# A new order for layer 0's hand-written table, and k's first product ahead of q's in layer 1

## The chip, the cores and the metric

The kernel runs on one core of a Trainium2 chip. The metric is the device time of one execution in microseconds (us). The engines are PE (TensorE, matrix products), DVE (VectorE), ACT (ScalarE), POOL (GpSimd) and SP (SyncE, which here only issues transfers). Each runs its own instructions in the order in which they were built, and waits for the others by semaphores.

## The reference, cut to what matters

Two transformer layers act on x of shape 4 x 512 x 512 in float32. Each is modulated by a row vector c:

```python
mod = (_silu(L0_c) @ L0_wmod).reshape(L0_c.shape[0], 6, 1, -1)
sa, ca, ga, sb, cb, gb = (mod[:, 0], mod[:, 1], mod[:, 2], mod[:, 3], mod[:, 4], mod[:, 5])
h = _layernorm(x, axis=-1) * (1 + ca) + sa
x = x + ga * _L0_attn_ref(h, L0_attn_Wq, L0_attn_bq, L0_attn_Wk, L0_attn_bk, L0_attn_Wv, L0_attn_bv)
h = _layernorm(x, axis=-1) * (1 + cb) + sb
x = x + gb * _L0_ffn_ref(h, L0_ffn_weight, L0_ffn_bias, L0_ffn_centroids, L0_ffn_assignments)
```

Layer 0's attention is small: a softmax over the 16 head dimensions of each position, whose result is repeated over 32 heads. Its feed-forward part computes softmax scores against 64 centroids and keeps a dense product only where a score passes a threshold. Layer 1 has the same frame with causal attention (32 query heads of 128, 8 key and value heads) and a gated feed-forward part with integer weights. Layer 1 takes most of the time.

## The kernel before, in words

All work is cut into tiles of 128 partitions. The batch has four entries b, and each entry's x is held on the chip as four tiles t of 128 rows. The schedule of layer 0 and of the start of layer 1 is manual: every engine gets its instructions in the order in which Python issues them.

**Layer 0** is a class `Pieces` (L291) with one short method per step, and a string `order` (L666) that lists the steps. A name such as `T.1.0.2` calls the method `T` with the numbers 1, 0, 2. `/d` or `/p` moves a step to DVE or POOL. The loop at L709 calls them one by one. Which engine a step uses:

- SP issues loads: `c`, `x.b` (x.0 alone from ACT), `wm.l.j` (the six 1 MB parts j of layer l's modulation weights, three buffers), `wq`, `wkv`, `cent`, `wffn`, `b2`, `asg`; `gw` and `gs` store a gate row and load it back, spread over all partitions; `wl` (L333) closes the buffers of modulation, opens those of layer 1 and loads its first q, k, v and o weights.
- PE: `M.l.j` multiplies silu(c) by a part of the weights; `MT` and `G` turn the result into columns (4 columns out) or a row; `T.i.b.c` transposes a normalized chunk; `Q.b.t` is the q, k, v product of 48 columns; `oT` and `ad` bring the attention back to x; `L` are the centroid scores; `hit` and `rs` collect the selection; `F.b.t` is the dense product, eight 512-column passes and the bias.
- DVE: `st` and `ve` and `nm` are the statistics of a layernorm; `wcat`, `bcat` sum weights and biases over heads; `biasr` splits the bias; `gr` clips a gate row; `qe`, `s`, `mx`, `den`, `rec`, `os`, `o` are the small attention; `xa`, `lm`, `ld`, `qs`, `fs`, `cs`, `sel` are adds, centroid softmax and selection; `mo` stores a modulation column.
- ACT: `siluexp`, `xn` (normalizing), `exp`, `le`, `re`; and, unless marked otherwise, the evacuations `pc`, `ev`, `oe`.
- POOL: `pw` (the power that gives 1/deviation), `sub` and `mul` of the attention, `R` (gate times a mask), `asgf`, `fa` unless marked, and `wsq` (sums of q's weights).

The last argument pairs are b and t, except that T and ev have a chunk c, and M, MT, pc, mo, G, gr, gw, gs have layer and part. The i of T, st, xn, ev and nm is 1 or 2 for layer 0's two layernorms and 3 for layer 1's first. M, `ad` and `F` share three banks of PSUM, `MT`, `G`, `Q`, `L` two others, and `T`, `oT` two more. A product that finds its bank unread waits for the step that empties it.

**Layer 1** multiplies 2 x 2 blocks by seven products (L738) in place of eight. They need sums of blocks of each operand: `sums_in` (L250) for weights, on POOL, and `sums_h` (L764) for h, on POOL and DVE (T1, T2, T3, T4 at L242 to L245). The products go in the order `SEVENTH = (1, 6, 2, 5, 3, 7, 4)`; product 1 needs no sum, 6 needs T2 and the weights' third sum, 7 needs T3. `gather` (L772) adds each product into q, k or v by DVE, product 1 by ACT. Products use the three banks of M and F. Eight pieces `select` (L278, `sel`) are spread between the first products, and `put` stores x to DRAM.

Attention then goes by `window` (L1120): each takes eight score tiles (products, row maxima, exponentials, division, flip), works pieces of other products in between, and ends with `carry` (L911), 16 transfers that turn the probabilities. Window -1 scores the first pair of heads and has no value products. The first half of q's two tiles, which it scores, is complete after the products 1, 6, 2, 5 and 3.

Of the kernel before, what the change touches and what calls it, by code (L numbers as in the profile page):

```python
# [33 lines left out]
def adaln_two_layers(ctx: ExitStack, tc: tile.TileContext, a, out: bass.AP):  # L34
# [629 lines left out]


    order = """  # L666
    c x.0 wkv wm.0.0 wq wm.0.1 x.2 wm.0.2 siluexp cent x.1 x.3 silu st.1.0.0 bcat st.1.0.1
    st.1.0.2 st.1.0.3 ve.1.0 pw.1.0 M.0.0 nm.1.0 xn.1.0.0 xn.1.0.1 wm.1.0 pc.0.0/d xn.1.0.2
    MT.0.0 xn.1.0.3 wcat T.1.0.0 mo.0.0 T.1.0.1 M.0.1 wm.0.3 pc.0.1/d MT.0.1 st.1.2.0
    st.1.2.1 mo.0.1 st.1.2.2 ev.1.0.0 st.1.2.3 T.1.0.2 ev.1.0.1 ve.1.2 pw.1.2 M.0.2  # L670
    ev.1.0.2/d nm.1.2 T.1.0.3 wm.0.4 pc.0.2/d b2 G.0.2 xn.1.2.0 ev.1.0.3/d xn.1.2.1 Q.0.0
    gr.0.2 xn.1.2.2 Q.0.1 xn.1.2.3 T.1.2.0 Q.0.2 st.1.1.0 ev.1.2.0 gw.0.2 T.1.2.1 st.1.1.1
    Q.0.3 ev.1.2.1 st.1.1.2 T.1.2.2 st.1.1.3 gs.0.2.0 gs.0.2.1 T.1.2.3 ev.1.2.2 qe.0
    gs.0.2.2 ve.1.1 gs.0.2.3 s.0 pw.1.1 ev.1.2.3 M.1.0 nm.1.1 mx.0 xn.1.1.0 Q.2.0 wm.1.3
    xn.1.1.1 pc.1.0/d asg sub.0 xn.1.1.2 Q.2.1 st.1.3.0 xn.1.1.3 st.1.3.1 MT.1.0 exp.0
    st.1.3.2 M.0.3 mo.1.0 st.1.3.3 Q.2.2 wm.1.4 pc.0.3 den.0 T.1.1.0 Q.2.3 ve.1.3 ev.1.1.0
    mul.0 rec.0 M.0.4 biasr MT.0.3 wm.0.5 pc.0.4 R.0 wffn T.1.1.1 os.0 T.1.1.2 ev.1.1.1 R.1
    ev.1.1.2 T.1.1.3 mo.0.3 R.2 o.0 MT.0.4 qe.2 ev.1.1.3 s.2 oT.0 R.3 Q.1.0 oe.0 mo.0.4 mx.2
    pw.1.3 ad.0.0 Q.1.1 nm.1.3 asgf xa.0.0 xn.1.3.0 sub.2 M.1.3 xa.0.1 xn.1.3.1 st.2.0.0
    xn.1.3.2 ad.0.1 wm.1.5 st.2.0.1 xn.1.3.3 Q.1.2 onehot exp.2 xa.0.2 T.1.3.0 xa.0.3 Q.1.3  # L680
    pc.1.3 den.2 ev.1.3.0 M.1.4 st.2.0.2 MT.1.3 mul.2 wm.1.2 pc.1.4 st.2.0.3 T.1.3.1 M.0.5
    rec.2 ev.1.3.1 ve.2.0 qe.1 pw.2.0 T.1.3.2 os.2 wm.1.1 pc.0.5 MT.1.4 ev.1.3.2 nm.2.0
    T.1.3.3 o.2 mo.1.4 xn.2.0.0 oT.2 s.1 G.0.5 ev.1.3.3 mo.1.3 xn.2.0.1 gr.0.5 Q.3.0
    xn.2.0.2 Q.3.1 xn.2.0.3 oe.2 T.2.0.0 ad.2.0 mx.1 gw.0.5 ev.2.0.0 T.2.0.1 xa.2.0 sub.1
    Q.3.2 ev.2.0.1 xa.2.1 gs.0.5.0 T.2.0.2 gs.0.5.1 st.2.2.0 ad.2.1 gs.0.5.2 ev.2.0.2
    gs.0.5.3 st.2.2.1 T.2.0.3 exp.1 xa.2.2 M.1.2 xa.2.3 ev.2.0.3 Q.3.3 den.1 pc.1.2 L.0.0
    st.2.2.2 mul.1 M.1.1 rec.1 st.2.2.3 L.0.1 pc.1.1 qe.3 ve.2.2 M.1.5 os.1 pw.2.2 L.0.2
    nm.2.2 o.1 xn.2.2.0 s.3 oT.1 MT.1.1 xn.2.2.1 oe.1/d L.0.3 xn.2.2.2 mx.3 xn.2.2.3 ad.1.0
    pc.1.5/d sub.3 T.2.2.0 lm.0 F.0.0 ev.2.2.0 xa.1.0 le.0 xa.1.1 exp.3 st.2.1.0 den.3
    T.2.2.1 st.2.1.1 mul.3 ad.1.1 ev.2.2.1 mo.1.1 rec.3 T.2.2.2 ld.0 G.1.5 ev.2.2.2 T.2.2.3  # L690
    xa.1.2 hit.0 ev.2.2.3 G.1.2 xa.1.3 F.0.1 os.3 st.2.1.2 st.2.1.3 o.3 ve.2.1 gr.1.5 pw.2.1
    oT.3 F.0.2 oe.3 nm.2.1 gw.1.5 qs.0 xn.2.1.0 fs.0.0 xn.2.1.1 fs.0.1 fa.0.0/p L.2.0
    xn.2.1.2 fs.0.2 xn.2.1.3 ad.3.0 fa.0.1/p fa.0.2/d T.2.1.0 xa.3.0 L.2.1 ev.2.1.0 xa.3.1
    T.2.1.1 st.2.3.0 ad.3.1 ev.2.1.1 st.2.3.1 T.2.1.2 xa.3.2 L.2.2 ev.2.1.2 xa.3.3 T.2.1.3
    st.2.3.2 L.2.3 ev.2.1.3 st.2.3.3 F.0.3 gr.1.2 ve.2.3 gw.1.2 lm.2 pw.2.3 L.1.0 fs.0.3
    le.2 F.1.0 nm.2.3 fa.0.3/p ld.2 xn.2.3.0 wl xn.2.3.1 qs.2 xn.2.3.2 xn.2.3.3 L.1.1
    T.2.3.0 L.1.2 ev.2.3.0/d T.2.3.1 L.1.3 ev.2.3.1/d T.2.3.2 lm.1 hit.2 ev.2.3.2 T.2.3.3
    F.1.1 ev.2.3.3/d le.1 ld.1 qs.1 fs.1.0 L.3.0 fa.1.0/d fs.1.1 hit.1 L.3.1 fa.1.1/d F.1.2
    L.3.2 fs.1.2 F.1.3 fa.1.2/d L.3.3 fs.1.3 F.2.0 fa.1.3/d lm.3 le.3 ld.3 F.2.1 qs.3 fs.2.0
    fa.2.0/d hit.3 fs.2.1 F.2.2 cs fa.2.1/p rs fs.2.2 F.2.3 re fa.2.2/d sel.0.0 sel.0.1  # L700
    sel.0.2 sel.0.3 F.3.0 st.3.0.0 st.3.0.1 st.3.0.2 st.3.0.3 fs.2.3 F.3.1 ve.3.0 fa.2.3/p wsq
    fs.3.0 fa.3.0/d pw.3.0 nm.3.0 sel.2.0 sel.2.1 sel.2.2 sel.2.3 xn.3.0.0 xn.3.0.1 F.3.2 fs.3.1 xn.3.0.2 fa.3.1/d xn.3.0.3
    T.3.0.0 fs.3.2 T.3.0.1 ev.3.0.0 F.3.3 fa.3.2/d ev.3.0.1 T.3.0.2 fs.3.3 T.3.0.3 ev.3.0.2
    fa.3.3/d ev.3.0.3
    """.split()
# [791 lines left out]
```

## Time and profile before

| | us |
|---|---|
| median of 3 runs | 2056.61 (2055.76 to 2058.26) |
| the profiled execution | 2058.11 |
| its span on the core | 2056.2 |
| PE busy in the span | 2020.9 |
| DVE, ACT, POOL busy | 1362.9, 878.9, 756.9 |
| first product M starts | 11.89 |
| last dense product of layer 0 (F.3.3) ends | 187.8 |
| first score product starts | 209.68 |
| first value product starts | 238.81 |

The span runs from the core's first to its last instruction. In rows of the timeline the first number is the start, the second the duration, and brackets hold the idle time of the engine ahead of the row and what ended it. Ends of matmuls are modelled, so a busy PE may still work below its peak. The granted clock is the share of TensorE's full clock; before its first recorded change the trace shows 1.00.

### The profile page before, as it was taken

To read this page: it belongs to the slowest core of one execution; us is meant where nothing else is said; L and a number is where in the kernel's file an instruction comes from. 1 tells how busy PE (TensorE), PEld (TensorE's weight loads), DVE (VectorE), ACT (ScalarE), POOL (GpSimd) and SP (SyncE) were. 2 spreads that over 40 slices of the span, in tenths; PEclk is the share of its full clock that TensorE was granted. 3 is DMA by queue.
4 is the path that set the end of the run, shared out by engine and by line. 5 is a ranking of instruction groups with operands and counts; after the bars stand their busy time and mean duration, and the time that the engine had idled before them with its cause. 6 is when DMAs were issued, how large, how long until landed. Compare 5 with 4: busy or idle time off the path is not lost.

```text
span 2056.2 us, 27492 instructions
## 1 busy us (share of the span) xinstructions
PE 2020.9 (98%) x9219; PEld 1580.4 (77%) x9219; DVE 1362.9 (66%) x3323; ACT 878.9 (43%) x1998; POOL 756.9 (37%) x656
## 2 busy tenths in 40 slices
PE   6999999999999999999999999999999999999998
PEld 4655777878787887877787878787877777888887
DVE  6766776677667666766677676667666674655554
ACT  3421554445444444544444445444444454223322
POOL 2314234434336443353473334337333333800000
PEclk8799999999999999999999999999999999999999
DMA  8310656676657766655766665567656556600000
GB/s 299 123 62 30 173 151 175 159 175 153 144 144 192 180 160 161 164 144 152 186 182 163 154 164 133 144 154 177 167 144 154 141 128 202 196 21 1 21 21 22
DMA packets 243640, 288.59 MB, mean 140 GB/s; under 512 B 23250, under 2 KB 184018, under 8 KB 243492
## 3 DMA queue, kind: packets, MB, share of 16 engines
q1 hardware_dynamic: 242964, 285.71, 52.8%
q8 instruction: 76, 1.25, 0.3%
q10 hardware_dynamic: 528, 1.05, 0.2%
q14 instruction: 72, 0.59, 0.1%
HBM read 142.99 MB, written 11.57 MB: 75 GB/s over the span
## 4 chain that ended last, share of the span: by engine, by line
PE 94%; DVE 3%; ACT 1%; issue 1%; DMA 1%; POOL 0%; SPq 0%; DVEq 0%; ACTq 0%
PE quarter L746 46%; PE av L928 14%; PE sc L878 13%; PE p_gate L1347 5%; PE p_up L1347 5%; PE acc L1366 4%; PE ffn L634 2%; PE lnT L477 1%; PE modps L390 1%; PE lg L593 1%; PE qkv_ps L507 1%; PE modT_ps L403 1%; PE add_ps L578 1%; DVE bnst L60 0%; DMA c_sb<-in_L_cT_dram 0%
## 5 line engine op out<-in xcount | busy, mean ns | idle before, releaser
L878 PE MATMUL sc<-kT,qT 128*128 128x512 f32 (+3 forms) x1024 | 355.1, 433 | 0.0
L928 PE MATMUL av<-x,v 128*128 128x512 f32 x1008 | 295.7, 437 | 3.7 <-DMA x<-p 3.7
L928 PEld LDWEIGHTS av<-x,v 128*128 128x128 f32 x1008 | 190.3, 192 | 110.7 <-issue 66.5
L881 DVE TENSOR_REDUCE nmx<-sc 128x1 f32<-128x512 f32 (+3 forms) x512 | 251.6, 491 | 17.7
L893 ACT ACTIVATE x<-x,rden 128x512 f32<-128x512 f32 (+3 forms) x256 | 143.6, 561 | 235.4 <-DVE rden L892 235.4
L778 DVE TENSOR_TENSOR qT<-qT,quarter 128x512 f32<-128x512 f32 x224 | 150.5, 684 | 133.9 <-PE quarter L746 127.7
L893 ACT ACTIVATE p<-p,rden 128x512 f32<-128x512 f32 (+3 forms) x256 | 143.7, 561 | 221.5 <-DVE rden L892 219.8
L879 DVE TENSOR_TENSOR sc<-sc,mask 128x128 f32<-128x128 f32 x512 | 145.5, 284 | 136.5 <-PE sc L878 135.6
L842 DVE TENSOR_TENSOR acc<-acc,quarter 128x512 f32<-128x512 f32 x196 | 134.5, 686 | 134.6 <-PE quarter L746 134.4
L230 POOL TENSOR_TENSOR sq<-wq 128x512 f32<-128x512 f32 x32 | 40.6, 1269 | 471.5 <-DMA wq<-in_L_attn_w_q_dram 453.0
L878 PEld LDWEIGHTS sc<-kT,qT 128*128 128x128 f32 x1024 | 182.6, 191 | 24.2
L746 PEld LDWEIGHTS quarter<-wo,oT 128*128 128x128 f32 x744 | 140.9, 190 | 43.9 <-issue 20.1
L746 PE MATMUL quarter<-wo,oT 128*128 128x256 f32 x744 | 171.1, 379 | 0.2 <-ACT oT L933 0.2
L883 ACT ACTIVATE p<-sc,nmx 128x512 f32<-128x512 f32 (+3 forms) x256 | 135.1, 528 | 75.8 <-DVE nmx L881 67.1
L883 ACT ACTIVATE x<-sc,nmx 128x512 f32<-128x512 f32 (+3 forms) x256 | 134.9, 527 | 70.1 <-DVE nmx L881 65.4
L933 ACT COPY oT<-av 128x512 f32<-128x512 f32 x128 | 74.3, 581 | 167.0 <-PE av L928 165.0
L896 DVE STREAM_TRANSPOSE p<-p 128x512 f32<-128x512 f32 (+3 forms) x256 | 129.4, 506 | 2.0 <-ACT p L893 0.5
L896 DVE STREAM_TRANSPOSE x<-x 128x512 f32<-128x512 f32 x248 | 125.0, 504 | 1.3 <-ACT x L893 0.9
L746 PE MATMUL quarter<-hsum,sq 128*128 128x256 f32 x512 | 121.1, 379 | 1.4 <-DVE hsum L244 1.4
L746 PEld LDWEIGHTS quarter<-hT,wq 128*128 128x128 f32 x512 | 97.2, 190 | 32.4 <-issue 14.8
L746 PE MATMUL quarter<-hsum,wq 128*128 128x256 f32 x512 | 121.0, 379 | 0.0
L746 PE MATMUL quarter<-hT,wq 128*128 128x256 f32 x512 | 120.9, 379 | 0.0
(257 smaller groups left out, 3752.7 us busy)
## 6 DMA issues: line engine op xcount, KB each, us to landing
x<-p SPq DMA_DIRECT2D x512, 128.0 KB, 3.7
x<-x SPq DMA_DIRECT2D x496, 128.0 KB, 3.8
wq<-in_L_attn_w_q_dram SPq DMA_DIRECT2D x32, 1024.0 KB, 5.6
...
```

Of the source, the lines that this page charges most:

```text
L746: nc.tensor.matmul(ps[:, m, :], l[:, k, m * P : (m + 1) * P], r[:, k, :], start=(k == 0), stop=(k == 1),)
L778: nc.vector.tensor_tensor(c[out], c[v], ps, ADD if sign > 0 else SUB)
L842: nc.vector.tensor_tensor(osum[:, i - 1], osum[:, i - 1], ps, ADD)
L878: nc.tensor.matmul(ps[:, :w], q[:, i * P : w], kT[n][:, :w], start=True, stop=True)
L879: nc.vector.tensor_tensor(ps[:, i * P : w], ps[:, i * P : w], mask, ADD)
L881: nc.vector.tensor_reduce(nmx, ps[:, :w], AX.X, ALU.max, negate=True)
L883: nc.scalar.activation(blocks(s, i), ps[:, :w].rearrange("p (j q) -> p j q", q=BK), AF.Exp, bias=nmx, accum_out=den,)
L893: nc.scalar.mul(p, p, rden)
L896: nc.vector.transpose(blocks(s, i), blocks(s, i))
L928: nc.tensor.matmul(av.rearrange("p (a n) -> p a n", a=NG)[:, :, BK * k :], vs[n][:, k, :], pT[:, k, :, P * (s % 2) + BK * k : P * (s % 2 + ...
L1347: nc.tensor.matmul(ps[kind], w[kind][:, k, c * P : (c + 1) * P], h2[b % 2][i][:, k, :], start=(k == 0 and i == 0), stop=(k == KC - 1 and i ...
L1366: nc.tensor.matmul(acc[t], act[i][:, t * P : (t + 1) * P], w[:, c, :], start=(n == 0 and i == 0), stop=(n == NI - 1 and i == 1),)
```

## The change

Layer 0's table is replaced by another order of the same steps. Two products M now come first on PE, several evacuations change engine, and tiles t are taken in other orders. The first F pieces come earlier and some at the very end, behind the normalizing for layer 1. `wl` comes later, and a new step `wsk` sums k's weights inside the table, where only `wsq` was. Two lines in `st` and `xn` open a buffer at the first tile taken, whichever it is.

In layer 1 the first products are k's first, q's first, the other six of k, four of q. The last two of q go into window -1, ahead of v's seven. The stores of x of entries 3, 0 and 1 are issued ahead of the next weights' loads, and k's load and sums ahead of q's.

```diff
@@ -341,6 +341,9 @@
             for kind in ("q", "k", "v", "o"):
                 load(kind, 0)
 
+        def wsk(self):
+            sums_in("k", 0)
+
         def wsq(self):
             sums_in("q", 0)
 
@@ -442,7 +445,7 @@
 
 
         def st(self, i, b, t):
-            if t == 0:
+            if ("st", i, b) not in T:
                 T["st", i, b] = moments()
             statistics(b, t, *T["st", i, b])
 
@@ -463,7 +466,7 @@
             )
 
         def xn(self, i, b, t):
-            if t == 0:
+            if ("xn", i, b) not in T:
                 pool = lnp if i == 3 else l0x
                 T["xn", i, b] = pool.tile([P, NT, E], F32, tag="xn" if i == 3 else f"xn{i}", name="xn", bufs=1)
             nc.scalar.activation(
@@ -664,44 +667,41 @@
 
 
     order = """
-    c x.0 wkv wm.0.0 wq wm.0.1 x.2 wm.0.2 siluexp cent x.1 x.3 silu st.1.0.0 bcat st.1.0.1
-    st.1.0.2 st.1.0.3 ve.1.0 pw.1.0 M.0.0 nm.1.0 xn.1.0.0 xn.1.0.1 wm.1.0 pc.0.0/d xn.1.0.2
-    MT.0.0 xn.1.0.3 wcat T.1.0.0 mo.0.0 T.1.0.1 M.0.1 wm.0.3 pc.0.1/d MT.0.1 st.1.2.0
-    st.1.2.1 mo.0.1 st.1.2.2 ev.1.0.0 st.1.2.3 T.1.0.2 ev.1.0.1 ve.1.2 pw.1.2 M.0.2
-    ev.1.0.2/d nm.1.2 T.1.0.3 wm.0.4 pc.0.2/d b2 G.0.2 xn.1.2.0 ev.1.0.3/d xn.1.2.1 Q.0.0
-    gr.0.2 xn.1.2.2 Q.0.1 xn.1.2.3 T.1.2.0 Q.0.2 st.1.1.0 ev.1.2.0 gw.0.2 T.1.2.1 st.1.1.1
-    Q.0.3 ev.1.2.1 st.1.1.2 T.1.2.2 st.1.1.3 gs.0.2.0 gs.0.2.1 T.1.2.3 ev.1.2.2 qe.0
-    gs.0.2.2 ve.1.1 gs.0.2.3 s.0 pw.1.1 ev.1.2.3 M.1.0 nm.1.1 mx.0 xn.1.1.0 Q.2.0 wm.1.3
-    xn.1.1.1 pc.1.0/d asg sub.0 xn.1.1.2 Q.2.1 st.1.3.0 xn.1.1.3 st.1.3.1 MT.1.0 exp.0
-    st.1.3.2 M.0.3 mo.1.0 st.1.3.3 Q.2.2 wm.1.4 pc.0.3 den.0 T.1.1.0 Q.2.3 ve.1.3 ev.1.1.0
-    mul.0 rec.0 M.0.4 biasr MT.0.3 wm.0.5 pc.0.4 R.0 wffn T.1.1.1 os.0 T.1.1.2 ev.1.1.1 R.1
-    ev.1.1.2 T.1.1.3 mo.0.3 R.2 o.0 MT.0.4 qe.2 ev.1.1.3 s.2 oT.0 R.3 Q.1.0 oe.0 mo.0.4 mx.2
-    pw.1.3 ad.0.0 Q.1.1 nm.1.3 asgf xa.0.0 xn.1.3.0 sub.2 M.1.3 xa.0.1 xn.1.3.1 st.2.0.0
-    xn.1.3.2 ad.0.1 wm.1.5 st.2.0.1 xn.1.3.3 Q.1.2 onehot exp.2 xa.0.2 T.1.3.0 xa.0.3 Q.1.3
-    pc.1.3 den.2 ev.1.3.0 M.1.4 st.2.0.2 MT.1.3 mul.2 wm.1.2 pc.1.4 st.2.0.3 T.1.3.1 M.0.5
-    rec.2 ev.1.3.1 ve.2.0 qe.1 pw.2.0 T.1.3.2 os.2 wm.1.1 pc.0.5 MT.1.4 ev.1.3.2 nm.2.0
-    T.1.3.3 o.2 mo.1.4 xn.2.0.0 oT.2 s.1 G.0.5 ev.1.3.3 mo.1.3 xn.2.0.1 gr.0.5 Q.3.0
...
-    fa.2.0/d hit.3 fs.2.1 F.2.2 cs fa.2.1/p rs fs.2.2 F.2.3 re fa.2.2/d sel.0.0 sel.0.1
-    sel.0.2 sel.0.3 F.3.0 st.3.0.0 st.3.0.1 st.3.0.2 st.3.0.3 fs.2.3 F.3.1 ve.3.0 fa.2.3/p wsq
-    fs.3.0 fa.3.0/d pw.3.0 nm.3.0 sel.2.0 sel.2.1 sel.2.2 sel.2.3 xn.3.0.0 xn.3.0.1 F.3.2 fs.3.1 xn.3.0.2 fa.3.1/d xn.3.0.3
-    T.3.0.0 fs.3.2 T.3.0.1 ev.3.0.0 F.3.3 fa.3.2/d ev.3.0.1 T.3.0.2 fs.3.3 T.3.0.3 ev.3.0.2
-    fa.3.3/d ev.3.0.3
+    wm.0.0 x.0 st.1.0.1 c st.1.0.3 st.1.0.2 siluexp st.1.0.0 wm.0.1 ve.1.0 pw.1.0 x.2 silu nm.1.0
+    x.1 M.0.1 st.1.2.0 xn.1.0.0 pc.0.1 M.0.0 st.1.2.1 MT.0.1 st.1.2.2 pc.0.0/d wkv mo.0.1 wm.0.2
+    st.1.2.3 xn.1.0.2 ve.1.2 xn.1.0.1 MT.0.0 wq xn.1.0.3 pw.1.2 T.1.0.0 mo.0.0 T.1.0.1 ev.1.0.0 b2
+    bcat ev.1.0.1 wm.0.3 wm.0.4 M.0.2 st.1.1.3 T.1.0.2 st.1.1.0 pc.0.2 ev.1.0.2 G.0.2 x.3 T.1.0.3
+    wcat nm.1.2 ev.1.0.3/d st.1.1.2 M.0.3 xn.1.2.0 xn.1.2.2 xn.1.2.3 st.1.1.1 gr.0.2 ve.1.1 pw.1.1
+    Q.0.0 xn.1.2.1 wm.1.0 Q.0.1 T.1.2.0 Q.0.2 T.1.2.1 wm.1.3 M.0.4 ev.1.2.0 st.1.3.1 ev.1.2.1
+    T.1.2.2 st.1.3.0 st.1.3.3 T.1.2.3 Q.0.3 ev.1.2.3 cent gw.0.2 nm.1.1 qe.0 gs.0.2.0 ev.1.2.2
+    M.1.0 s.0 wm.1.4 Q.2.0 mx.0 st.1.3.2 sub.0 Q.2.1 xn.1.1.0 pc.1.0 xn.1.1.1 MT.1.0 Q.2.2 biasr
+    pc.0.4 xn.1.1.3 xn.1.1.2 mo.1.0 R.0 exp.0 wm.0.5 T.1.1.0 Q.2.3 ev.1.1.0 den.0 T.1.1.1 mul.0
+    qe.2 s.2 ve.1.3 asg pc.0.3 gs.0.2.2 ev.1.1.1 MT.0.3 os.0 MT.0.4 rec.0 o.0 oT.0 oe.0 mx.2
+    mo.0.3 T.1.1.2 mo.0.4 ev.1.1.2/d pw.1.3 sub.2 ad.0.0 T.1.1.3 exp.2 M.1.3 xa.0.0 xa.0.1
+    ev.1.1.3 nm.1.3 den.2 ad.0.1 xn.1.3.0 xn.1.3.2 gs.0.2.1 Q.1.0 xn.1.3.1 mul.2 st.2.0.0 rec.2
+    xa.0.3 xn.1.3.3 xa.0.2 asgf Q.1.1 M.1.4 pc.1.4 R.2 Q.1.2 T.1.3.0 ev.1.3.0 wm.1.5 Q.1.3 os.2
+    st.2.0.3 o.2 st.2.0.2 st.2.0.1 qe.1 oT.2 s.1 mx.1 wm.1.2 M.0.5 wffn MT.1.4 mo.1.4 pc.0.5
+    T.1.3.1 sub.1 G.0.5 gs.0.2.3 oe.2 wm.1.1 ve.2.0 T.1.3.2 pc.1.3 ev.1.3.1 gr.0.5 M.1.5 ev.1.3.2
+    MT.1.3 mo.1.3 gw.0.5 exp.1 den.1 rec.1 pc.1.5 pw.2.0 mul.1 T.1.3.3 ad.2.0 M.1.2 nm.2.0
+    ev.1.3.3 xn.2.0.0 Q.3.0 xa.2.0 pc.1.2 xa.2.1 xn.2.0.2 G.1.5 Q.3.1 xn.2.0.3 st.2.2.0 xn.2.0.1
+    os.1 R.1 ad.2.1 Q.3.2 st.2.2.1 o.1 T.2.0.0 xa.2.2 ev.2.0.0 xa.2.3 oT.1 Q.3.3 T.2.0.1 oe.1
+    ad.1.0 T.2.0.2 st.2.2.2 qe.3 st.2.2.3 ev.2.0.1 xa.1.1 s.3 ve.2.2 ev.2.0.2 xa.1.0 T.2.0.3
+    ad.1.1 pw.2.2 xa.1.3 nm.2.2 ev.2.0.3 gs.0.5.0 mx.3 xa.1.2 L.0.0 xn.2.2.0 M.1.1 xn.2.2.2
+    st.2.1.2 xn.2.2.3 xn.2.2.1 L.0.1 R.3 F.0.3 L.0.2 sub.3 gs.0.5.2 st.2.1.0 T.2.2.0 st.2.1.1
+    L.0.3 gr.1.5 pc.1.1 lm.0 exp.3 st.2.1.3 T.2.2.1 le.0 den.3 ld.0 ev.2.2.0 ev.2.2.1 ve.2.1 F.0.1
+    T.2.2.2 G.1.2 rec.3 mul.3 os.3 pw.2.1 T.2.2.3 o.3 F.0.0 ev.2.2.2 nm.2.1 hit.0 ev.2.2.3 qs.0
+    oT.3 xn.2.1.0 fs.0.3 xn.2.1.3 L.2.0 oe.3 fs.0.1 fs.0.0 xn.2.1.1 xn.2.1.2 ad.3.0 gs.0.5.3
+    xa.3.0 L.2.1 T.2.1.0 L.2.2 ad.3.1 xa.3.3 L.2.3 T.2.1.1 xa.3.1 F.0.2 lm.2 xa.3.2 le.2 st.2.3.3
+    st.2.3.2 ev.2.1.1 T.2.1.2 st.2.3.1 st.2.3.0 F.2.2 ev.2.1.2 ve.2.3 pw.2.3 gw.1.5 ld.2 fa.0.1/d
+    T.2.1.3 nm.2.3 ev.2.1.0 xn.2.3.0 F.2.0 qs.2 xn.2.3.3 xn.2.3.2 xn.2.3.1 ev.2.1.3/d T.2.3.0
+    L.1.0 fs.0.2 T.2.3.1 fa.0.0 F.2.1 ev.2.3.0 gr.1.2 T.2.3.2 fs.2.2 hit.2 ev.2.3.1 fa.0.2/d
+    fa.0.3/d ev.2.3.2/d T.2.3.3 L.1.1 gw.1.2 ev.2.3.3 L.3.0 fa.2.2 L.1.2 L.3.1 L.1.3 F.2.3
+    gs.0.5.1 onehot L.3.2 lm.1 MT.1.1 le.1 ld.1 fs.2.0 L.3.3 hit.1 lm.3 le.3 F.3.0 ld.3 hit.3
+    fs.2.1 fs.2.3 F.3.2 qs.3 mo.1.1 fs.3.0 qs.1 cs fa.3.0/d fa.2.0/d rs fa.2.3/d re sel.0.2 fs.3.2
+    F.1.1 sel.0.3 F.3.1 st.3.0.3 fa.2.1 sel.0.0 sel.0.1 F.1.2 st.3.0.1 st.3.0.2 st.3.0.0 sel.2.1
+    sel.2.3 ve.3.0 pw.3.0 sel.2.0 fs.1.1 fa.3.2/d wl wsk nm.3.0 fs.1.2 F.1.3 xn.3.0.0 wsq fa.1.2/d
+    fs.3.1 xn.3.0.1 xn.3.0.3 xn.3.0.2 T.3.0.0 T.3.0.2 ev.3.0.2 F.1.0 T.3.0.3 ev.3.0.0/d fs.1.0
+    sel.2.2 T.3.0.1 fa.1.1 fs.1.3 ev.3.0.1/d ev.3.0.3/d F.3.3 fa.1.3 fs.3.3 fa.3.3 fa.3.1 fa.1.0
@@ -1155,21 +1155,23 @@
     run(*put(2, x[2]))
     sums_h(0, (nc.gpsimd, nc.vector))
     nc.gpsimd.memset(prob2[0], 0.0)
-    sums_in("k", 0)
     sums_in("v", 0)
     sums_wo(0)
     others = select_pieces(3) + select_pieces(1)
-    for piece in q_pieces(0) + k_pieces(0):
+
+    q, k = q_pieces(0), k_pieces(0)
+    for piece in k[:1] + q[:1] + k[1:] + q[1:5]:
         piece()
         if others:
             others.pop(0)()
+    q_rest = q[5:]
+    run(*put(3, x[3]), *put(0, x[0]), *put(1, x[1]))
+    load("k", 1)
     load("q", 1)
-    load("k", 1)
+    sums_in("k", 1)
     sums_in("q", 1)
-    sums_in("k", 1)
-    run(*put(3, x[3]), *put(0, x[0]), *put(1, x[1]))
     q = q_pieces(1)
-    window(-1, v_pieces(0))
+    window(-1, q_rest + v_pieces(0))
     load("v", 1)
     pending = []
     begun = []
```

More of the change, by code (lines that the diff above doesn't have):

```diff
@@ L679, in adaln_two_layers @@
-    pw.1.3 ad.0.0 Q.1.1 nm.1.3 asgf xa.0.0 xn.1.3.0 sub.2 M.1.3 xa.0.1 xn.1.3.1 st.2.0.0
-    xn.1.3.2 ad.0.1 wm.1.5 st.2.0.1 xn.1.3.3 Q.1.2 onehot exp.2 xa.0.2 T.1.3.0 xa.0.3 Q.1.3
-    pc.1.3 den.2 ev.1.3.0 M.1.4 st.2.0.2 MT.1.3 mul.2 wm.1.2 pc.1.4 st.2.0.3 T.1.3.1 M.0.5
-    rec.2 ev.1.3.1 ve.2.0 qe.1 pw.2.0 T.1.3.2 os.2 wm.1.1 pc.0.5 MT.1.4 ev.1.3.2 nm.2.0
-    T.1.3.3 o.2 mo.1.4 xn.2.0.0 oT.2 s.1 G.0.5 ev.1.3.3 mo.1.3 xn.2.0.1 gr.0.5 Q.3.0
-    xn.2.0.2 Q.3.1 xn.2.0.3 oe.2 T.2.0.0 ad.2.0 mx.1 gw.0.5 ev.2.0.0 T.2.0.1 xa.2.0 sub.1
@@ L685, in adaln_two_layers @@
[L685 to L696, printed above, removed]
@@ L697, in adaln_two_layers @@
-    T.2.3.0 L.1.2 ev.2.3.0/d T.2.3.1 L.1.3 ev.2.3.1/d T.2.3.2 lm.1 hit.2 ev.2.3.2 T.2.3.3
-    F.1.1 ev.2.3.3/d le.1 ld.1 qs.1 fs.1.0 L.3.0 fa.1.0/d fs.1.1 hit.1 L.3.1 fa.1.1/d F.1.2
-    L.3.2 fs.1.2 F.1.3 fa.1.2/d L.3.3 fs.1.3 F.2.0 fa.1.3/d lm.3 le.3 ld.3 F.2.1 qs.3 fs.2.0
-    fa.2.0/d hit.3 fs.2.1 F.2.2 cs fa.2.1/p rs fs.2.2 F.2.3 re fa.2.2/d sel.0.0 sel.0.1
-    sel.0.2 sel.0.3 F.3.0 st.3.0.0 st.3.0.1 st.3.0.2 st.3.0.3 fs.2.3 F.3.1 ve.3.0 fa.2.3/p wsq
-    fs.3.0 fa.3.0/d pw.3.0 nm.3.0 sel.2.0 sel.2.1 sel.2.2 sel.2.3 xn.3.0.0 xn.3.0.1 F.3.2 fs.3.1 xn.3.0.2 fa.3.1/d xn.3.0.3
```

## The prediction

> **What bounds the kernel now.** I read the page first: TensorE is named busy throughout, and its clock dips only at the start.
>
> ```profile
> PE 2020.9 (98%) x9219; PEld 1580.4 (77%) x9219; DVE 1362.9 (66%) x3323; ACT 878.9 (43%) x1998; POOL 756.9 (37%) x656
> PEclk8799999999999999999999999999999999999999
> ```
>
> The edit lies in the first 240 us of 2056, so only that stretch can pay directly. Next the windows (columns: length; busy time and count of PE, PEld, DVE, ACT, POOL; granted clock; DMA):
>
> ```profile
> 36.00:38.00 2.00, 2.00 (x20) 1.86 (x16) 1.22 (x2) 0.18 (x1) 1.89 (x1) 1.00 0.09 22
> 38.00:40.00 2.00, 0.04 (x1) 0.00 (x0) 1.89 (x4) 1.64 (x3) 0.59 (x2) 0.79 0.88 236
> 40.00:42.00 2.00, 1.94 (x12) 1.92 (x16) 1.93 (x6) 1.84 (x3) 1.42 (x1) 0.50 0.84 256
> ...
> 76.00:78.00 2.00, 2.00 (x17) 1.39 (x14) 0.00 (x0) 1.20 (x2) 0.00 (x0) 0.82 0.37 108
> ```
>
> The clock halves in one window and returns in the other. Means of 0.79 and 0.82 put the drop at 39.2 and the return at 76.7. TensorE's timeline shows the price: the same four matmuls of a modulation product (piece M) in both states, and the pieces around the return.
>
> ```profile
> 35.06 1.06 PE L390 MATMUL modps<-wm,silu_c 128*32 128x512 f32 x8
> 40.06 1.87 PE L403 MATMUL modT_ps<-diag,part 128*128 128x4 f32 x8 [2.02 <-DVE part L286]
> 56.09 0.45 PE L567 MATMUL oT_ps<-ident,o 128*128 128x128 f32 x1
> 73.72 1.09 PE L477 MATMUL lnT<-ident,xn 128*128 128x128 f32 x4
> 74.75 1.94 PE L390 MATMUL modps<-wm,silu_c 128*32 128x512 f32 x8
> 187.30 0.50 PE L638 MATMUL ffn<-bias_r,ones_r 2*128 2x512 f32 x1
> 191.91 1.96 PE L746 MATMUL quarter<-hsum,sq 128*128 128x256 f32 x8 [1.35 <-DVE hsum L244]
> ```
>
> The bracketed 2.02 us at 40.06 precedes the halved clock. From there to 181 no row of TensorE shows a wait: layer 0 runs at TensorE's pace, first at half speed. So moving a DVE wait out of that stretch is worth little by itself; the clock and the two ends decide. At the hand-over the waits of TensorE (reason: sum, times, longest), and DVE's timeline, read:
>
> ```profile
> PE av L928 <- DMA x<-p: 3.7, 1, 3.7
> PE quarter L746 <- DVE hsum L244: 1.4, 1, 1.4
> PE quarter L746 <- DVE kT L780: 1.1, 1, 1.1
> ```
> ```profile
> 44.90 2.20 DVE L370 CAST b_hi<-b 2x512 fp32r<-2x512 f32 x1
> 52.35 0.23 DVE L561 TENSOR_TENSOR o<-os,den 128x64 f32<-128x64 f32 x1
> 189.23 0.69 DVE L243 TENSOR_TENSOR hsum<-hT 128x512 f32<-128x512 f32 x1
> 190.02 1.73 DVE L244 TENSOR_TENSOR hsum<-hT,hsum 128x512 f32<-128x512 f32 x1
> 224.63 0.31 DVE L896 STREAM_TRANSPOSE p<-p 128x128 f32<-128x128 f32 x1 [0.47 <-ACT p L893]
> ```
>
> The last row ends the first window of scores; its carry follows and sets the 3.7 us wait of the first av product.
>
> [...] the window 73.3-76.7 (1.0 us of transposes, 1.9 of M) opened the clock; 69.9-73.3 (1.9 of M, 1.2 of MT) did not. [...]
>
> **The change part by part.** The order is written by hand and the built program follows it on every engine; no work of layer 0 is added or lost. Some evacuations change between DVE and ACT: pc.0.1, pc.0.2, pc.1.0 and ev.1.0.2 (2.9 us) leave DVE in front of o.0. Durations per piece from TensorE's rows, clock open / halved: M 0.99/1.9, MT 0.82/1.8, T 0.55/1.0, Q 0.9/1.8, ad 1.06/2.0, G 0.95/1.9, F 3.87 open. The halved G has no row: 0.95 if it did not slow, 2.0 by doubling; I take 1.9.
>
> *Start.* The first transfers are now 1 MB pieces. In the windows 10-36 the DMA moved 0.38 MB per us. Behind wm.0.0, x.0 and wm.0.1 the first M starts at about 12.3 (before 11.89): no gain. Then M.0.1 and M.0.0 come together, x.2, x.1, wm.0.2 and wq land by 23.5, so wcat (2.28 us) ends near 26 instead of 17.5; this delay stays hidden, since Q.0.0 also needs T.1.0.3 and M.0.3, ending near 28.5. Before, Q.0.0 began at 29.7. Q.0.3 ends at about 35 (34.1 before, with two M fewer ahead of it), and DVE takes qe.0 at 35.6, as before.
>
> *To oT.0.* From qe.0 DVE sets the pace: qe 0.35, s 1.23, mx 1.21, one st 0.87, biasr 6.2 as before, where POOL worked beside it, or 4.5 without that, den 1.2, qe.2 and s.2 1.6, os 1.2, rec 0.5, o 0.2, and about 0.6 of small ones: 13.5 to 15.2 us, so o.0 ends at 49.1 to 50.8. I take oT.0 at 50.0, 6.1 us earlier. SP's ga row and POOL's R.0 (1.3) and mul.0 (2.4) end near 44, below this chain. TensorE has only M, MT, four Q, T, T, MT, MT in that time, 8.2 us open. I therefore expect low windows there and a halved clock again, as before.
>
> *Halved stretch.* From oT.0 the order is T ad T M ad Q Q M Q T Q oT M MT T G T, then M.1.5. At half clock: five T 5.0, two ad 4.0, three M 5.7, four Q 7.2, oT 0.3, MT 1.8, G 1.9 = 25.9, to 75.9. The run T G T M is the first long one (5.8 us of halved time); I let the clock return there, at 75.9. Before, it returned at 76.7.
>
> *Open stretch.* Before had 187.8 - 76.7 = 111.1 us left to F.3.3's end, 1.4 of it idle: 109.7. At 75.9 the new order has done one T, one G, one oT more (1.7), but runs two T.3.0 (1.0) ahead of F.3.3: 109.0. I add 0.5 for F.3.2, whose bank waits for fs.2.1 behind ld.3. End: 185.4, a gain of 2.4. F.3.3 and F.1.0 moved behind xn.3.0, but the old order already had F under sel, st and POOL's rstd, so this fills only the 1.4 us of xn waits, counted in the 111.1. pw.3.0 is now ahead of both weight sums on POOL; if xn were late, F.1.1 to F.1.3 (15.6) cover its chain of about 13.7.
>
> *wl.* The four loads (3 MB, 8 us) now stand behind MT.1.1's buffer; four F and more cover them, and wsk (3.4) and wsq (5.5). Without that cover TensorE would wait 8 plus 3.4. Behind them on POOL stand five fa (6.3) and T3 of hsum; T3 is due at the sixth k product, about 6.6 us after F.3.3. T3 ends near 6-7: nothing, or 0.5.
>
> *Hand-over.* F.3.3's end to the last flip was 224.95 - 187.84 = 37.1. Now: products k0 0.87 and q0 1.73 run during fs.3.3 0.75, T1 and T2 (0.69 to 1.73 each against POOL), so k1 starts at 3.3 instead of 4.1 after two T and one q. The k products (0.87) are shorter than sel plus one gather step on DVE (0.73 + 0.41), so the three banks make TensorE wait about 1.6 over k2 to k6. q1 to q4 end at 17.0. The old window took 224.95 - 209.68 = 15.3 from there; q7 and q4 add three DVE steps of 0.68, 2.0. Sum 34.3 to 34.6; gain 2.6. Bounds: 4.2 without a bank wait, 0 if sel contends at 1.2 us each. Stores of x now precede load k1, load q1 on SP. q1 is issued after the last q0 product, about 22 after F.3.3, lands at 27.5 (5.3 before), and its third sum on POOL ends at 31.4; its user comes at 33: hidden, up to 3 us if not. The carry's 16 issues and the av wait follow the last flip unchanged.
>
> Sum: -2.4 - 2.6 = -5.0. Made on the profiled execution (span 2056.2, the other 1.9 of its 2058.11 around it) it gives 2053.1; that run lies 1.5 above the median 2056.61, so 2051.6 for the median.
>
> **Rivals.** *Early return of the clock* (likeliest case 0.45, this 0.25): T.1.1.3 and M.1.3, 2.9 us together, open it near 56.2. The 19.7 us from there to 75.9 become about 10.2 and all moves 9.5 more: 2042, or 2045 where DVE then holds TensorE. For: the same pair opened it before. Against: it needs the right phase. *Late return* (0.15), the slower one: [...] MT, ad, Q and L follow until F.0.3, the first 3.9 us product. That is 17 us of open work run twice as long: +17 - 5.0, 2068.6. It decides as soon as the clock stays halved 10 us beyond 75.9, which costs the whole gain. For: M plus ad, 3.9 us at 61.9-65.8, did not open it before. *Waits take the gain* (0.15): oT.0 comes later than 50, or F.0.3, F.0.1 and F.0.0 hold the three banks until their fs, which stand some 20 us of DVE work later, in front of ad.3.0. DVE was 97% busy at 80-110. Margin by my count 1 us, so 2-6 us lost: about 2056. That the change doesn't do what it says I exclude by the built order: M.0.1 is TensorE's first work, k's first product directly follows F.3.3.
>
> **How the numbers follow.** Within 0.2% (4.1 us) is about what a measurement here cannot tell from no change. Of the likeliest case, 2047 to 2056 alone, three quarters are faster by more. Faster: 0.34 + 0.25 + 0.02 = 0.61; same: 0.10 + 0.09 = 0.19; slower: 0.15 + 0.05 = 0.20. The range 2041 to 2066 takes in the early case down to its centre and leaves out most of the late one: some 0.1 at each end.
>
> **What would show it.** oT at 49-51 (right start); granted clock halved from about 42 to 76 (likeliest), to 56 or past 86 (rivals); F.3.3's end near 185; 34 to 35 us from it to the first carry; the 1.35 and 1.06 us waits gone or under 1 each. Wrong if TensorE waits at ad.3.0, at F.3.0 to F.1.0 or for sq, or if windows after 240 differ.

## The result and the profile after

The changed kernel takes 2043.52 us in the median of nine executions (2040.46 to 2051.95), the kernel before 2056.61 (2054.01 to 2058.88). The ratio is 0.9946, with a 95% interval of 0.9930 to 0.9963: 13 us faster. The nine times fall into two groups, five from 2040.5 to 2043.5 and four from 2048.7 to 2052.0. A second run of the same kernel (*after_again* below) adds three to each, so there is a profile of either group: one of 2043.52 us (span 2041.6), called *early*, and one of 2049.72 us (span 2047.7), called *late*. The granted clock of all fifteen executions splits in the same way: 0.990 to 0.994 in the eight lower times, 0.986 to 0.989 in the seven upper ones. The kernel before has one group.

The page of the early one, TensorE's line and its clock, reads almost as before; 15 us in 2056 do not show in 40 slices:

```profile
PE 2006.0 (98%) x9219; PEld 1571.0 (77%) x9219; DVE 1363.2 (67%) x3317; ACT 878.8 (43%) x2001; POOL 759.5 (37%) x659
PEclk8999999999999999999999999999999999999999
```

The windows show it (columns as in the prediction: length; busy time and count of PE, PEld, DVE, ACT, POOL; granted clock; DMA). First the early profile:

```profile
38.00:40.00 2.00, 2.00 (x21) 2.00 (x20) 1.97 (x4) 2.00 (x4) 1.60 (x1) 1.00 0.14 24
40.00:42.00 2.00, 2.00 (x15) 2.00 (x14) 1.89 (x4) 1.68 (x4) 0.34 (x1) 0.64 0.83 114
...
56.00:58.00 2.00, 2.00 (x12) 0.51 (x4) 1.71 (x4) 2.00 (x4) 1.43 (x1) 0.59 0.03 1
58.00:60.00 2.00, 2.00 (x18) 1.75 (x16) 1.60 (x3) 0.65 (x1) 2.00 (x3) 1.00 0.89 246
```

and the late one, of the same program:

```profile
38.00:40.00 2.00, 2.00 (x14) 2.00 (x13) 1.97 (x4) 2.00 (x4) 1.44 (x1) 0.60 0.15 27
...
56.00:58.00 2.00, 2.00 (x8) 0.51 (x4) 1.66 (x4) 2.00 (x4) 1.49 (x1) 0.50 0.03 5
...
74.00:76.00 2.00, 2.00 (x6) 0.72 (x4) 0.69 (x2) 0.28 (x1) 0.72 (x1) 0.51 0.67 259
76.00:78.00 2.00, 2.00 (x18) 1.03 (x17) 1.93 (x3) 1.76 (x3) 0.00 (x0) 1.00 0.00 0
```

From the partial means (0.64 and 0.59; 0.60 and 0.51) the clock is halved from 40.6 to 57.6 in the early execution and from 38.4 to 76.0 in the late one. Before, it was halved from 39.2 to 76.7. The shortest halved stretch in the early profile's trace, 183.92 to 187.34, is 3.413 us long, and in each of the fourteen profiles all changes of the clock from 14 to 250 us lie whole multiples of this apart, within 0.05 us. A step of that length is called a window of the clock below: the early stretch is five of them, the late one eleven. From oT.0 to 57 us TensorE's timeline has the same instructions at the same times in both. Early, then late:

```profile
50.66 0.45 PE L570 MATMUL oT_ps<-ident,o 128*128 128x128 f32 x1 [3.81 <-DVE o L564]
...
53.90 1.11 PE L480 MATMUL lnT<-ident,xn 128*128 128x128 f32 x4
54.95 1.94 PE L393 MATMUL modps<-wm,silu_c 128*32 128x512 f32 x8
56.81 1.51 PE L581 MATMUL add_ps<-ga,oT 32*128 32x512 f32 x4
58.25 1.99 PE L510 MATMUL qkv_ps<-wcat,h1n 128*128 128x48 f32 x16
...
175.09 0.49 PE L641 MATMUL ffn<-bias_r,ones_r 2*128 2x512 f32 x1
```
```profile
53.85 1.11 PE L480 MATMUL lnT<-ident,xn 128*128 128x128 f32 x4
54.89 1.94 PE L393 MATMUL modps<-wm,silu_c 128*32 128x512 f32 x8
56.76 2.08 PE L581 MATMUL add_ps<-ga,oT 32*128 32x512 f32 x4
58.77 3.65 PE L510 MATMUL qkv_ps<-wcat,h1n 128*128 128x48 f32 x16
...
73.40 1.87 PE L418 MATMUL gateps<-part,diag 128*4 128x512 f32 x2
75.20 1.00 PE L480 MATMUL lnT<-ident,xn 128*128 128x128 f32 x4
...
183.61 0.49 PE L641 MATMUL ffn<-bias_r,ones_r 2*128 2x512 f32 x1
...
234.08 4.55 PE L928 MATMUL av<-x,v 128*128 128x512 f32 x16 [1.68 <-DMA x<-p]
```

T.1.1.3 and M.1.3 run at 53.9 and 54.9 in both. What differs is where the windows of the clock lie against this work; this is called the phase below. Counted back in steps of 3.413 from each return, one window of the early execution is 54.2 to 57.6 and holds M.1.3 whole with 0.8 us of T and 0.8 of ad; those of the late one are 52.1 to 55.5 and 55.5 to 58.9, and their border cuts M.1.3. Two other profiles with the same table up to there agree: early_adds has a window from 53.9 to 57.3, which holds M.1.3 whole, and the clock returns at its end; table_only has windows that meet at 55.4, inside M.1.3, and it stays halved to 75.9. So F.3.3 ends at 175.6 or at 184.1 (before 187.8). At the hand-over TensorE's longest wait from 170 to 245 us is now 2.6 us for `gather`; the one for hsum, 1.4 before, has shrunk to 0.4, and the one of the first av product from 3.7 to 1.7 (late profile: sum, times, longest):

```profile
PE quarter L746 <- DVE kT L780: 2.6, 1, 2.6
PE av L928 <- DMA x<-p: 1.7, 1, 1.7
```

A table of all landmarks, the last flip being the one ahead of the first carry:

| | before | early | late | table_only | start_only | early_adds |
|---|---|---|---|---|---|---|
| F.3.3's end, us | 187.8 | 175.6 | 184.1 | 183.8 | 187.1 | 175.6 |
| from there to the last flip | 37.1 | 37.6 | 36.2 | 35.5 | 34.8 | 34.5 |
| from there to the first av | 13.9 | 14.0 | 13.7 | 13.6 | 13.5 | 13.5 |
| from there to the end | 1817.4 | 1814.4 | 1813.6 | 1816.4 | 1815.5 | 1813.4 |
| span | 2056.2 | 2041.6 | 2047.7 | 2049.3 | 2050.9 | 2036.9 |

### The profile page after: what moved, and what is told of

The parts are those of the page before. It is cut to its first block, busy times and chain, and to the rows that moved or that the text cites. A ratio compares the mean times of both kernels' runs of the same rounds, so it can differ in the third digit from the quotient of the medians.

```text
span 2041.6 us, 27493 instructions
## 1 busy us (share of the span) xinstructions
PE 2006.0 (98%) x9219; PEld 1571.0 (77%) x9219; DVE 1363.2 (67%) x3317; ACT 878.8 (43%) x2001; POOL 759.5 (37%) x659
## 4 chain that ended last, share of the span: by engine, by line
PE 89%; DVE 1%; ACT 1%; SPq 0%; DMA 0%; issue 0%; ACTq 0%
PE quarter L746 47%; PE av L928 14%; PE sc L878 13%; PE p_gate L1349 5%; PE p_up L1349 5%; PE acc L1368 5%; PE lnT L1035 0%; PE lnT L1314 0%; SPq L918 0%; DMA x<-p 0%; DVE nmx L881 0%; ACT x L883 0%; DVE x L1377 0%; ACT tm L1089 0%; DVE tm L1376 0%
```

## The experiments

Theory *clock*: the gain is the shorter halved stretch, by phase, and the new start of layer 1 adds nothing, since 37.6 is no less than 37.1. Rivals: the start gains it, or DVE's shorter chain to oT.0.

**One part alone.** *table_only* keeps the old start behind the new table; *start_only* is the old table with wsk in it and the new start. Only the main lines of both edits are shown.

```diff
-    q, k = q_pieces(0), k_pieces(0)          # table_only
-    for piece in k[:1] + q[:1] + k[1:] + q[1:5]:
+    for piece in q_pieces(0) + k_pieces(0):
...
-    fs.3.0 fa.3.0/d pw.3.0 nm.3.0 ...        # start_only
+    fs.3.0 fa.3.0/d pw.3.0 wsk nm.3.0 ...
...
```

> The new table (with the sums of wk as its piece wsk) and the old start of layer 1. Theory 'clock' (the gain is the halved clock ending near 57 instead of 76.7, and the new start of layer 1 gains nothing): median 2040 to 2051, F.3.3 ends near 175 where the clock returns near 57, and F.3.3's end to the last flip is 37 to 38. Theory 'start' (the new start gains the 2.6 us that I forecast, or more): 2046 to 2056, with 40 us from F.3.3's end to the last flip.

> The old table with wsk behind pw.3.0, where GpSimd is idle for 10 us, and the new start of layer 1. Theory 'clock': halved from 39.2 to 76.7 as before, F.3.3's end near 187.8, and 36 to 38 us from there to the last flip: 2055 to 2059. My forecast's second term taken at its word: 34.5 us there, 2054. Theory 'start': 2050 or below.

table_only: 2050.35 us (2041.8 to 2052.2, six executions), ratio 0.9962 (0.9943 to 0.9980), in the same two groups, 2041.8 to 2044.4 and 2050.0 to 2052.2; its profile is of the late kind (38.4 to 75.9). start_only: 2052.47 us (2050.6 to 2061.5, twelve), ratio 0.9989 (0.9979 to 0.9998), its clock halved from 40.4 to 74.6. The table carries the two groups and, group by group, most of the gain: its times lie within 2 us of the changed kernel's. But the start is not worth nothing: in the old table it takes the hand-over to 34.8 (my forecast for the new one was 34.3 to 34.6), and the av product comes with a wait of 1.5 instead of 3.7 us. In the new table the same start is 0.7 slower to the last flip than the old one (36.2 against 35.5). So something in the new table holds it up.

**The same kernel again.**

> The changed kernel as it is. Theory 'clock': two groups of times again, 2040 to 2045 where the clock returns near 57 and 2048 to 2052 where it stays halved to about 75, and the profile shows the one that fits its own time. Rival: the second group comes from something behind 240 us, and the clock returns near 57 in both.

2049.72, 2051.35, 2042.16, 2043.97, 2049.61, 2043.38: two groups again, and the profiled one, of the upper group, has the clock halved to 76.0. What lies behind the av product takes as long in both profiles (1814.4 and 1813.6). The rival falls.

**Filler ahead of oT.0.** A piece wa(n) of n further matmuls, spread over the stretch that ends at oT.0 (*warm*: eight; *warm_two*: two), and seven in the kernel before (*before_warm*).

```diff
+        def wa(self, n):
+            for _ in range(n):
+                nc.tensor.matmul(hits_ps, ident, x[0][:, 0, :], start=True, stop=True)
-    ... MT.0.3 os.0 MT.0.4 rec.0 o.0 oT.0 ...
+    ... MT.0.3 wa.2 os.0 MT.0.4 wa.2 rec.0 o.0 oT.0 ...  # warm, and four more wa.1
+    ... MT.0.3 os.0 MT.0.4 wa.2 rec.0 o.0 oT.0 ...       # warm_two
```

> The changed kernel with eight further matmuls of TensorE, 128x128 by 128x512 into an unused bank, spread over the pieces from Q.2.0 to oT.0, where TensorE waits 3.8 us; their results are not used. Theory 'clock': no halved window between 40 and 58; seven to eight us of halved time come back and the spread of the times shrinks: 2034 to 2040, oT.0 still at 50.5 because DVE sets it. Rival 'DVE' (what was gained is DVE's shorter chain, the clock only follows): 2043 to 2050 with or without halved windows; if the further matmuls do not count for the clock, they cost 7 us or more halved: 2048 to 2056.

> The kernel before with seven of the same further matmuls between Q.2.0 and MT.0.3, two of them in the 2.02 us wait ahead of MT.1.0. Theory 'clock': the clock stays open at 39.2 or comes back before 50; some 18 us of halved time come back less 6 us for the further matmuls, and less what DVE then holds: 2040 to 2050, so most of the table's gain appears without the new table. Rival 'DVE' (the new table's order of DVE's work is what was gained): 2054 to 2063.

> The changed kernel with two of the further matmuls only, directly ahead of oT.0, in its wait of 3.8 us (3.5 us at the halved clock). The earlier run with eight showed no halved window and the same F.3.3 end (175.5), so the halved time ahead of oT.0 costs nothing and only what follows it counts. Theory 'clock': the window that ends near 50.8 becomes a busy one, the clock is open again between 50 and 54.5, F.3.3 ends at 172 to 175.5, and the slow group is gone: 2037 to 2043. If one such window is not enough: two groups as in the changed kernel.

warm: 2041.76 us (2040.2 to 2045.6, four executions), no halved window from 25.7 to 138.3 us, and yet F.3.3 ends at 175.5, as in the early profile. My seven to eight us did not come: oT.0 still comes at 50.8, since o.0 on DVE ends only at 50.5, so only the halved time behind oT.0 counts, 7 us of it in the early profile, 3.5 us of loss; of that a wait of 0.7 and a halved window at 138.3 to 141.7 (1.7) took most back. One of the four (2045.58) had a granted clock of 0.993 against 0.996 and 0.997 and may be of an upper group. before_warm: 2052.87 us (2046.7 to 2055.5), ratio 0.9976, between both forecasts; it held the clock open to 55.6, then lost it to 72.6. warm_two: 2044.06 us (2040.9 to 2052.9), both groups. Its profiled execution is one of 2052.86 us, and shows why two are too few. The clock was still open there, so the two were done in 2 us, and a wait of 3.1 us followed (timeline, then windows):

```profile
45.03 1.96 PE L400 MATMUL hits_ps<-x,ident 128*128 128x512 f32 x4
50.07 0.30 PE L574 MATMUL oT_ps<-ident,o 128*128 128x128 f32 x1 [3.08 <-DVE o L568]
```
```profile
46.00:48.00 2.00, 0.99 (x3) 0.16 (x1) 1.99 (x2) 0.00 (x0) 1.96 (x1) 1.00 1.06 381
48.00:50.00 2.00, 0.00 (x0) 0.00 (x0) 1.97 (x4) 0.00 (x0) 1.01 (x1) 1.00 0.97 240
50.00:52.00 2.00, 1.93 (x7) 1.17 (x9) 1.96 (x4) 0.27 (x1) 0.86 (x1) 0.59 0.09 33
```

The clock fell at 50.4 and stayed halved to 77.7.

**The hand-over.** DVE in the early profile, then GpSimd, with the three adds fa.3.3, fa.3.1 and fa.1.0, which stand behind fs.3.3 in the table, and T3 (L242) behind them:

```profile
178.72 1.64 DVE L245 TENSOR_TENSOR hsum<-hsum,hT 128x512 f32<-128x512 f32 x1
180.28 3.47 DVE L280 COPY_PREDICATED x<-rsel,hT 128x512 f32<-128x512 uint32 x2
183.65 0.40 DVE L780 SCALAR_TENSOR_TENSOR kT<-quarter,kT 128x256 f32<-128x256 f32 x1
```
```profile
176.87 4.62 POOL L651 TENSOR_TENSOR hT<-hT,x 128x512 f32<-128x512 f32 x3 [2.69 <-DVE hT L644]
181.45 1.72 POOL L242 TENSOR_TENSOR hsum<-hT 128x512 f32<-128x512 f32 x1
```

Two select instructions take 1.79 and 1.78 us there, one directly behind the other. I took it that they wait for fa.3.1, whose result the second one reads. The trace does not show this: fa.3.1 had ended at 179.8, and no idle time stands in front of either. They are slow while GpSimd adds beside them. In the fourteen profiles all 129 select instructions without an addition of GpSimd beside them take 0.70 to 0.74, those beside its memset too; each of the 57 that take more than 0.76, up to 1.82, has at least 0.6 us of such additions beside it. Of the three adds only fa.3.3 needs F.3.3. *early_adds* turns the order on GpSimd:

```diff
-    ... F.3.3 fa.1.3 fs.3.3 fa.3.3 fa.3.1 fa.1.0
+    ... F.3.3 fa.1.3 fa.3.1 fa.1.0 fs.3.3 fa.3.3
```

> The changed kernel with GpSimd's fa.3.1 and fa.1.0 ahead of fs.3.3 and fa.3.3 in the table, so that they need not wait for F.3.3. Theory: the 2.55 us wait of the sixth k product is that of select(3,1) for GpSimd's late fa, and of T3 behind it; it falls to 0 to 0.5, and F.3.3's end to the first av product goes from 51.6 to 48.5 to 49.5; times 2 to 2.5 us lower in each group (2038 to 2043 and 2046 to 2050). Rival: eight select and the gather steps are simply too much for DVE there; the wait stays at 1.6 or more and the stretch at 50.5 or more.

2038.44 us (2036.9 to 2046.6, six executions), ratio 0.9932 (0.9914 to 0.9949), in two groups, each 3 to 5 us below those of the changed kernel. DVE, TensorE's waits from 170 to 245 us, GpSimd:

```profile
180.42 1.35 DVE L280 COPY_PREDICATED x<-rsel,hT 128x512 f32<-128x512 uint32 x2
```
```profile
PE quarter L746 <- DVE hsum L244: 0.6, 1, 0.6
PE quarter L746 <- DVE kT L780: 0.4, 1, 0.4
```
```profile
172.88 5.40 POOL L651 TENSOR_TENSOR hT<-hT,x 128x512 f32<-128x512 f32 x4 [2.85 <-DVE hT L644]
178.23 1.72 POOL L242 TENSOR_TENSOR hsum<-hT 128x512 f32<-128x512 f32 x1
179.89 3.51 POOL L1157 MEMSET p<- 128x4096 f32 x1
```

GpSimd is done with its additions at 179.95, and its memset runs beside the two select instructions, which now take 0.73 and 0.72. The wait is 0.4 and the stretch 34.5, so it was this order, though not by the dependency that I had expected. That is 2.1 of the 4.7 us between the spans of the two early profiles. The rest fits the clock again: the changed kernel's had halved windows at 183.9 to 187.3, upon the 2.55 us wait, and at 228.3 to 231.7; this one has none.

**Filler behind M.1.3, and both kinds with the adds.** *fill_adds* is early_adds with `wa.2` (here on x of entry 1) directly behind M.1.3; *warm_two_adds* and *warm_adds* are the fillers of above with early_adds.

> The kernel early_adds with two of the further matmuls directly behind M.1.3 (3.5 us at the halved clock, 1.8 open). Together with T.1.1.3 and M.1.3 they make 6.5 us of halved work at full width, nearly two windows, so one whole window is busy whatever the phase. Theory 'phase' (the two groups are whether a window falls on T.1.1.3 and M.1.3): one group, clock back at 54 to 61 in all, 2037 to 2042, the upper group near 2046 gone. Rival 'two full windows needed' or another cause: two groups, each 2 us above those of early_adds (2039 and 2048).

> Both edits together. If both theories hold they add up: 2035 to 2041, one group of times, F.3.3's end to the first av product 48.5 to 49.5. If only one holds, 2037 to 2043 with one group or 2038 to 2050 with two.

> Eight further matmuls ahead of oT.0, as in warm, with the adds of early_adds. If both edits add up: one group, 2036 to 2041, with F.3.3's end to the first av product near 48. If the clock's phase still decides behind oT.0: two groups, with one near 2046.

fill_adds: 2040.23 to 2042.00 in five of five, median 2040.72, ratio 0.9931 (0.9918 to 0.9943), clock back at 58.1. That is what phase asks for, at a price of 2 to 3 us against the lower group of early_adds. Five even times are weak evidence by themselves: with the shares of early_adds, two upper times in six, five lower ones in a row come by chance about once in eight. warm_two_adds: 2041.73 us (2039.0 to 2042.8), one group in five executions; its clock had fallen at 38.7, the two fillers took 3.8 us halved and put oT.0 at 53.3. warm_adds: 2046.43 us (2037.0 to 2059.7, nineteen), two groups, nine up to 2039.8 and ten from 2046.4. So filler ahead of oT.0 does not remove the upper group, and the four times of warm were too few to show that it had gone. warm_two's profile shows the clock falling behind the filler, at 50.4; of warm_adds' upper group there is only the granted clock, 0.985 to 0.993 against 0.996 to 0.999 in the lower one.

**Making oT.0 earlier, and real work as filler.** *mul_first_adds* takes biasr and R.0 out of the chain to oT.0; *pair_adds* puts M.1.4 behind M.1.3. Both start from early_adds.

```diff
-    Q.2.2 biasr ... mo.1.0 R.0 exp.0 ... mul.0 ... mo.0.4 ev.1.1.2/d       # mul_first_adds
+    Q.2.2 ... mo.1.0 exp.0 ... mul.0 R.0 ... mo.0.4 biasr ev.1.1.2/d
-    M.1.3 xa.0.0 ... rec.2 xa.0.3 ... Q.1.1 M.1.4 pc.1.4 R.2               # pair_adds
+    M.1.3 M.1.4 xa.0.0 ... rec.2 pc.1.4 xa.0.3 ... Q.1.1 R.2
```

> The kernel early_adds with two edits on the chain to oT.0: biasr moved from ahead of den.0 to behind mo.0.4, and mul.0 ahead of R.0 on GpSimd, since R.0 waited for its row until 44.4 us and mul.0 stood behind it until 48.5 to 48.8. If this chain sets oT.0: os.0 no longer waits 2.3 us for GpSimd, oT.0 at 47 to 48.5 instead of 50.7, and 2 to 3 us less in each group (2035 and 2044). If TensorE's halved work, which ends near 46.9 to 48.3, sets it then: 0 to 2 us. Rival: biasr in its new place delays the evacuations behind it by its 3.4 us: no gain or slower.

> The kernel early_adds with no further work, but M.1.4 moved from behind Q.1.1 to directly behind M.1.3 (and its copy pc.1.4 ahead of the fourth xn.1.3 on ScalarE). T.1.1.3, M.1.3 and M.1.4 are then 5.0 us of halved work in one piece, against 3.05 in early_adds and 6.5 in fill_adds. Theory 'phase': the upper group near 2046 gets rare or goes, and what stays is 2037 to 2040, since no work is added. If M with its 32 columns of weights, or 5.0 us, is not enough to fill a window in every phase: two groups, 2037 to 2039 and 2045 to 2047. Rival: ad.0.1 waits for a bank until pc.1.4 is done; the window then falls idle as in mul_first_adds, 2046 to 2050 in most.

mul_first_adds: 2048.8 us (2046.8 to 2049.9), one group, the upper one. oT.0 came at 49.35, 1.5 earlier than in early_adds, and the clock opened at 54.9. But biasr, on DVE until 54.4, delayed xa.0.0, and ad.0.1 waited for it:

```profile
53.62 1.67 PE L393 MATMUL modps<-wm,silu_c 128*32 128x512 f32 x8
55.80 1.72 PE L581 MATMUL add_ps<-ga,oT 32*128 32x512 f32 x4 [0.50 <-DVE x L587]
57.45 2.89 PE L510 MATMUL qkv_ps<-wcat,h1n 128*128 128x48 f32 x16
```

The window 54.9 to 58.3 held the wait, ad and Q, and the clock fell again until 75.4. pair_adds: 2047.59 us (2041.1 to 2049.1), four of five in the upper group. The clock opened at 58.8, and the next window, with M.1.4 gone from between the Q, held ad and Q alone:

```profile
58.00:60.00 2.00, 2.00 (x8) 0.79 (x4) 0.00 (x0) 1.30 (x2) 2.00 (x3) 0.80 0.86 274
60.00:62.00 2.00, 2.00 (x17) 1.82 (x17) 1.71 (x3) 0.00 (x0) 0.28 (x1) 1.00 1.02 375
62.00:64.00 2.00, 2.00 (x13) 2.00 (x13) 1.97 (x5) 0.00 (x0) 0.00 (x0) 0.55 1.03 374
```

TensorE is busy 2.00 of 2.00 there, and the clock falls at 62.2 all the same. My expectation had looked at what opens the clock, and not at what keeps it open. Both of these readings were made after the fact.

## Why the prediction was right, and where not

The forecast was 2051.6 us with faster as the likeliest sign; 2043.52 lies inside the range of 2041 to 2066. Two of its cases are what happens, one per execution. By their times, seven of fifteen are the likeliest case, halved to 76 (2048.7 to 2052), and eight are *Early return*, near 57 (2042 forecast, 2040.5 to 2044 measured). That these are two phases of one kernel and not two possible kernels I had not seen, so I put 0.45 and 0.25 where the shares are about one half each. Which group holds the median is luck: it is 2043.52 with five lower times of nine and 2046.79 with three of six.

*Start*: right where it mattered. The first M at 13.3 and not 12.3 (it waited for silu on DVE), wcat's end at 27.2 and not 26, both hidden: Q.0.0 began at 28.6, qe.0 at 35.5.

*To oT.0*: 50.7 for 50.0, by luck, since two errors cancel. biasr took 3.4 us and not 4.5 to 6.2, but "SP's ga row and POOL's R.0 (1.3) and mul.0 (2.4) end near 44, below this chain" failed. In the early profile the row came at 44.3, R.0 took 1.9, and mul.0 stood behind it until 48.5; os.0 waited 2.3 us for it. In the late profile mul.0 ended at 47.5, and DVE waited 2.5 us for TensorE's Q.2.3 instead. The sum had counted TensorE's pieces there at 8.2 us, with the clock open, though it expected the clock halved. Early, then late:

```profile
48.58 1.22 DVE L561 TENSOR_REDUCE os<-s 128x64 f32<-128x1024 f32 x1 [2.31 <-POOL s L552]
```
```profile
46.50 0.36 DVE L518 TENSOR_TENSOR qkv<-qkv_ps,bcat 128x192 f32<-128x192 f32 x1 [2.52 <-PE qkv_ps L510]
```

*Halved stretch*: 75.9 forecast, 76.0 measured in the late profile, in the run named: the window 72.5 to 75.9 holds 1.6 us of T and all of G (1.87, taken as 1.9). That the return comes there was my estimate from the order of work; the returns at 57.6 and 76.0, behind the same instructions from oT.0 on, show that it varies from one execution to the next.

*Open stretch*: 108.1 us from 76.0 to F.3.3's end, 109.5 forecast; no wait for F.3.2. F.3.3 gained 3.7 for 2.4 in the late case. The clock returns there only 0.7 us earlier than before, after eleven halved windows in both, so these 3.7 us are the table's order and not the early return. DVE's shorter chain to oT.0 (50.6 for 56.1) may be what gains them; no run separates it from the rest of the order.

*Hand-over*: mis-sized, for the changed kernel. 36.2 measured, 34.3 to 34.6 forecast, a gain of 0.9 for 2.6. k1's 3.3 us were right. The term "the three banks make TensorE wait about 1.6 over k2 to k6" measured 2.55 in one wait, since I costed the select instructions at 0.73 and two of them took 1.8 beside GpSimd's additions. The bound "0 if sel contends at 1.2 us each" had named this. On POOL I had looked only for when T3 ends ("nothing, or 0.5"), not for what runs beside the five fa ahead of it. With that order changed the stretch is 34.5. So two of the named signs failed: 34 to 35 us to the first carry, and the two waits "gone or under 1 each" (0.4 and 2.55).

*The av wait* "follows the last flip unchanged": the time does (13.9 and 13.7), its effect does not. Before, TensorE waited 3.72 us there, the clock was halved from 237.1 to 244.0, and the first av products took 7.1 us:

```profile
238.81 7.10 PE L928 MATMUL av<-x,v 128*128 128x512 f32 x16 [3.72 <-DMA x<-p]
```

In the late profile the wait is 1.68, no window is halved and the row takes 4.55. All three profiles with the old start, with waits of 3.4 to 3.7 us, have halved windows there; of the eleven with the new start, with waits of 1.3 to 2.1, one has. From the last flip to the end this is 4.0 us less in the late profile; 6.8 us of halved time account for at most 3.4 of it. I had named windows after 240 that differ as a sign of being wrong, and those up to 244 do differ. So the late case is -3.7 -0.9 -4.0 = -8.6 on the span, where I had -2.4 -2.6.

*Late return* did not happen to the changed kernel; warm_two's 77.7 was the latest. *Waits take the gain*: no wait of TensorE at ad.3.0 or F in either profile.
